# Placing the output scatters of the last layer of a four-layer graph network

## The chip, the cores and the metric

One core of one Trainium2 chip runs the whole kernel as one program. The metric is the device time of one execution in microseconds (us); the time before is the median of three executions, 2123.89 us.

## The reference, cut to what matters

The input x holds 16 samples of 1024 nodes with 128 features, adj is a 1024 x 1024 adjacency matrix in which about 0.8% of the entries are set. Four layers follow each other. Layers 0, 2 and 3 are attention over the neighbours of a node with 8 heads of 16 features, then a residual, a layer norm, a two-layer feed-forward of width 256, a residual and a layer norm. Layer 1 is graph attention with one score per edge.

```python
def attention(adj, h):                        # layers 0, 2, 3
    Q, K, V = h @ Wq, h @ Wk, h @ Wv          # 8 heads of 16
    scores = where(adj == 0, -inf, Q K^T / 4)
    o = softmax(scores) V
    x = layer_norm(h + o @ Wo + bo)
    return layer_norm(x + relu(x @ W1 + b1) @ W2 + b2)

def graph(adj, x):                            # layer 1
    h = x @ W
    e = leaky_relu((h @ a_src)[i] + (h @ a_dst)[j])
    return layer_norm(softmax(where(adj == 0, -inf, e)) @ h + x)
```

## The kernel before

**Tiling.** The graph is sparse, so the kernel gathers the neighbours of a node and does not multiply with the whole matrix. At the start (graph, slots) it sorts the nodes by degree and makes lists of neighbours. A layer is cut into 16 blocks: two groups g of 8 samples, and for each of them eight sets t of 128 nodes (in four quarters of 32). The list units holds the 64 blocks of all layers in order; a block is called by its index there, so blocks 48 to 63 are the last layer.

**Parts.** A block of an attention layer has five parts. A part is one or two chunks; a chunk is one gather of 128 table rows (4 neighbours for each of 32 nodes), and a row holds keys and values of 8 samples, 8 KB. The five parts have 2, 2, 2, 1 and 2 chunks. The one chunk of the fourth part mixes neighbours of all quarters that were left over. Sets t = 1 and t = 4 have pairs whose two chunks belong to the same quarter.

**The loop.** The loop over i goes through all 288 parts in order. begun is the index of a block's first part, so that i == begun + 3 is its fourth. In an iteration i of an attention layer the instructions are issued in this order:

- products(i), L985: VectorE multiplies the gathered keys with the queries, 128 x 2048 for two chunks. In the fourth part GpSimd does it instead (product_of_shared, L1000), issued two iterations ahead.
- summed(i - 2), L1062: TensorE sums the weighted values of neighbours into the nodes. In the second part of a block, divided starts for the block before (the denominators, also L1062).
- exponentials(i): VectorE sums over the 16 features of a head (L1018), ScalarE takes exponentials (L1022).
- weighted(i - 1), L1046: VectorE multiplies values with exponentials, in the same buffer.
- gathered(i - 1 + AHEAD) with AHEAD = 4, L971: GpSimd issues the indirect DMAs of the part three ahead, into one of four buffers e, the one that weighted(i - 1) has just read.
- product_of_shared(i + 2) on GpSimd, if that is a fourth part.
- all output scatters that stand in the list ready, on GpSimd (L702). Behind them the small addition of the sums to seen (L1115), in the iteration after the division.
- in the second part: the division of the block before (L1099, L1102 on VectorE), which makes its two tails, one for each half h of 4 samples.

**Tails.** A tail (attention_tail, then finish) does the output projection, the norms and the feed-forward of one half on TensorE and ScalarE, in small steps that are put between the parts above by a plan written out by hand (PLANS). It starts in the second part of the block after its own and is done in the second part of the next. At its end in the last layer, finish turns the half into the tile outs (two buffers, tag kv), and when the second half is there it puts one scatter of both halves into ready: 128 rows of 4 KB to the places of the nodes in out.

**The end.** The tails of block 63, the last, run after the loop with nothing beside them; half 1 uses VectorE where half 0 uses ScalarE. finish scatters each half by itself (L695), with the row numbers in halves, which are made at the start (L394). The scatter of block 62 is issued after the loop as well, ahead of block 63's tails.

**Queues.** All indirect DMAs are issued from GpSimd's queue in program order; the plain ones (x from kept, qx from qr) from SyncE's.

Of the kernel before, what the change touches and what calls it, by code (L numbers as in the profile page):

```python
# [16 lines left out]
I32 = mybir.dt.int32  # L17
AF = mybir.ActivationFunctionType
ALU = mybir.AluOpType
# [3 lines left out]
P = 128  # L23
# [20 lines left out]
T = N // P  # L44
GR = 2
G = B // GR
HF = 2
# [97 lines left out]
def sparse_path(ctx: ExitStack, tc: tile.TileContext, a: dict, out: bass.AP, flag):  # L145


    nc = tc.nc
    const = ctx.enter_context(tc.tile_pool(name="const", bufs=1))
# [25 lines left out]
    def rep_of(j, whole=False):  # L175
# [6 lines left out]
            name=nc.get_next_instruction_name(), act_func_set_id=BOTH,  # L182
# [9 lines left out]
    marks = const.tile([P, len(MARK), 32], F32, name="marks")  # L192
    nc.gpsimd.memset(marks, 0.0)
    places = const.tile([P, GR, T], I32, name="places")
    halves = const.tile([P, HF], I32, name="halves")
    bad = const.tile([P, T], F32, name="bad")
    seen = const.tile([P, 2, G * H], F32, name="seen")
    nc.gpsimd.memset(seen, 0.0)
# [37 lines left out]
    def graph(wide):  # L236
# [146 lines left out]
        there = s1.tile([P, T], F32, name="there")  # L383
# [5 lines left out]
        for g in range(GR):  # L389
            nc.vector.tensor_scalar(  # L390
                places[:, g, :], there, float(GR), float(g), ALU.mult, ALU.add,
            )
        for h in range(HF):
            nc.vector.tensor_scalar(  # L394
                halves[:, h : h + 1], there[:, T - 1 :], float(GR * HF), float((GR - 1) * HF + h),
                ALU.mult, ALU.add,
            )
        low = s1.tile([P, T], F32, name="low")
        nc.vector.tensor_tensor(bad, sorted_[:, :, 2], caps[:, :T], ALU.is_gt)
# [251 lines left out]
    def turned(z, dst, gain=None, shift=None, dve=False):  # L651

        ps = bank([P, GH, P])
        for i in range(GH):
            nc.tensor.transpose(ps[:, i, :], z[:, i, :], ident)  # L655
        if dve and gain is None:
            nc.vector.tensor_copy(dst, ps)
        elif dve:
            nc.vector.tensor_scalar(dst, ps, gain, shift, ALU.mult, ALU.add)
        elif gain is None:  # L660
            nc.scalar.copy(dst, ps)  # L661
        else:
            nc.scalar.activation(dst, ps, AF.Identity, bias=shift, scale=gain)  # L663
# [5 lines left out]
    ready = []  # L669

    def finish(l, g, t, h, z, gain, shift, dve=False):
        if l + 1 < len(LAYERS):

            wanted[0] = True
            while held[0]:
                advance(slow)
            wanted[0] = False
            busy[0] += 1
            xn = states.tile([P, GH, P], F32, tag="xT", name="xT")
            turned(z, xn, gain, shift)  # L680
            yield "free"
            yield from project(l + 1, g, t, h, xn)
            busy[0] -= 1
            return
        xn = states.tile([P, GH, P], F32, tag="xT", name="xT")
        turned(z, xn, gain, shift, dve)
        yield
        if h == 0:
            leaving[g, t] = twos.tile([P, HF, GH, D], F32, tag="kv", name="outs")
        o = leaving[g, t]  # L690
        turned(xn, o[:, h], dve=dve)
        yield
        yield
        if (l, g, t) == units[-1]:
            nc.gpsimd.indirect_dma_start(  # L695
                out=out.rearrange("n (k c) -> (n k) c", k=GR * HF),
                out_offset=bass.IndirectOffsetOnAxis(ap=halves[:, h : h + 1], axis=0),
                in_=o[:, h].rearrange("p g d -> p (g d)"), in_offset=None,
            )
        elif h + 1 == HF:  # L700
            rows = o.rearrange("p h g d -> p (h g d)")
            ready.append(lambda: nc.gpsimd.indirect_dma_start(  # L702
                out=out.rearrange("n (k c) -> (n k) c", k=GR),
                out_offset=bass.IndirectOffsetOnAxis(ap=places[:, g, t : t + 1], axis=0),
                in_=rows, in_offset=None,
            ))

    def hidden():
        return ones_.tile([P, F * GH * P], F32, tag="f1", name="f1")
# [157 lines left out]
    units = [(l, g, t) for l in range(len(LAYERS)) for g in range(GR) for t in range(T)]  # L867
# [10 lines left out]
    def is_attention(u):  # L878
        return LAYERS[units[u][0]][1] is ATTN
# [244 lines left out]
    def advance(gens):  # L1124
        for gen in list(gens):
            got = next(gen, "end")
            if got == "end":
                gens.remove(gen)
            elif got == "free":
                free.append(gen)  # L1130
# [58 lines left out]
    with tc.manual_schedule():  # L1189
        wide = [gather_buffer() for _ in range(EDGES)]  # L1190
        setup, entry, weights = graph(wide), at_once(0), load_weights("L0")
        next(setup)
        next(weights)
# [39 lines left out]
        begun = 0  # L1233
        slot = ()
        for i in range(len(parts) + 2):
            here = i < len(parts)
            u = parts[i][0] if here else len(units)
            if here:
                l = units[u][0]
                eager[0] = 1 if u < 2 else 0  # L1240
                if i and parts[i - 1][0] != u:
                    begun = i
                    if u == 1:
                        fronts.append(ends)
                    if l + 1 < len(LAYERS) and LAYERS[l + 1][1] is ATTN:
                        if units[u][1:] == (0, 1):
                            more = load_weights(LAYERS[l + 1][0])
                            next(more)
                            next(more)
                        if units[u][1:] == (0, 4):  # L1250
                            fronts.append(more)
                if is_attention(u):
                    products(i)
            if i > 1:
                summed(i - 2)
                done = parts[i - 2][0]
                if parts[i - 1 : i] == [] or parts[i - 1][0] != done:
                    closing = divided(done)
                    next(closing)
            if here and i == begun and is_attention(u):  # L1260
                shared(u)
            if here and (i == 5 or i == begun + 3 and 0 < u < T - 2):
                slot = islice(rest, 1)
                fronts.insert(0, slot)
            others()
            if here:
                exponentials(i)
                if i in (1, 6) or i == begun + 4 and 0 < u < T - 2:
                    for _ in slot:
                        pass  # L1270
                    for _ in islice(rest, 1):
                        pass
            if here and i == begun + 1:
                while loads:
                    advance(loads)
                if u + 1 < len(units):
                    fronts.insert(0 if u else len(fronts) - 1, queries(u + 1))
                loads.append(loaded(u + 2))
                if u:
                    advance(loads)  # L1280
            others()
            if 0 < i <= len(parts):
                weighted(i - 1, 0)
                if not is_attention(parts[i - 1][0]):
                    others()
                    weighted(i - 1, 2)
                gathered(i - 1 + AHEAD)
                product_of_shared(i + 2)
                while ready:
                    ready.pop(0)()  # L1290
                for _ in sizes:
                    pass
            if closing is not None and here:
                while any(gen not in free for gen in tails):
                    if opening[0] is None:
                        advance(tails)
                    else:
                        planned("ab")
                while opening[0] is not None and opening[0] < len(plan[0]):
                    planned()  # L1300
                next(closing)
                sizes, closing = closing, None
                passes = 3 if is_attention(u) else 4
                steps = STEPS if is_attention(done) else GRAPH_STEPS
                steps -= LATE[units[done][0]]
                pace[:] = 0.0, steps / (passes * sum(part[0] == u for part in parts) - 1)
                if is_attention(done) and opening[0] is None:
                    for gen in list(tails):
                        if gen in free:
                            for _ in gen:  # L1310
                                pass
                            tails.remove(gen)
                opening[0] = 0 if is_attention(done) else None
                plan[0] = PLANS.get(units[done][0], ())
            others()
            if i + 1 >= len(parts) or parts[i + 1][0] != u:

                while fronts:
                    advance(fronts)
# [445 lines left out]
```

## Time and profile before

| what | value |
|---|---|
| median of three executions | 2123.89 us (2122.29 to 2125.0) |
| the profiled execution | 2126.89 us |
| its span, first to last instruction | 2125.0 us |
| TensorE busy | 1972.9 us, 93% |
| VectorE busy | 1806.1 us, 85% |
| ScalarE busy | 1519.5 us, 72% |
| GpSimd busy | 1182.4 us, 56% |
| moved by DMA | 636.10 MB, 299 GB/s on average |
| gathers L971 | 576, 1523 ns of GpSimd each on average |
| scatters L702 | 15, 3060 ns of GpSimd in the median |
| scatters L695 | 2, 978 ns of GpSimd in the median |

In the views PE is TensorE, DVE VectorE, ACT ScalarE, POOL GpSimd; L702 is line 702 of the kernel. A timeline line gives the start in us, the duration in us, the engine, the line, the operation with its tiles as output<-inputs, and in brackets how long the engine stood idle before it and what ended that. The time of an indirect DMA on POOL is that of issuing it; the data move later. A line of the view by windows gives the window, its length, the busy us and instruction count of PE, weight loads, DVE, ACT and POOL, then the granted TensorE clock, the share of time that the DMA engines were busy, and GB/s.

### The profile page before, as it was taken

Reading aid. Unit: us, or ns where it says so; the run is one execution under the profiler, and the core shown is the slowest. Engines: PE = TensorE matmul, PEld = TensorE weight load, DVE = VectorE, ACT = ScalarE, POOL = GpSimd, SP = SyncE. Lnnn points to the kernel's source line nnn. Section 1 sums busy time; section 2 is a strip of 40 time slices with the busy share of each in tenths; the row PEclk is TensorE's granted clock in tenths of the full one; section 3 lists DMA queues with packets and bytes.
Section 4 is the critical chain, followed back from the end, with each engine's and each line's share of the span. In section 5 each row is a group of like instructions: output and inputs, shape, how many; then the busy total and the mean of one; then the engine's idle time right before and its main releaser. Section 6 shows DMA issues by size and latency. Waiting matters only on the chain.

```text
span 2125.0 us, 37303 instructions
## 1 busy us (share of the span) xinstructions
PE 1972.9 (93%) x13444; PEld 1244.8 (59%) x13444; DVE 1806.1 (85%) x1315; ACT 1519.5 (72%) x5051; POOL 1182.4 (56%) x747
## 2 busy tenths in 40 slices
PE   7689999999999999998899999999999999999986
PEld 6455665656666555554466665666656565565554
DVE  6977989999997577677899999999998898989892
ACT  3347878878786555555587887878888777777763
POOL 4344555556555488784454555555566565656550
PEclk8789999999999999999999999999999999999998
DMA  8987888889888799998899999999988878698860
GB/s 275 340 302 260 319 302 303 315 285 316 318 309 292 233 355 356 328 357 315 304 326 328 328 337 316 326 325 338 333 314 281 301 262 305 238 314 282 298 217 22
DMA packets 164800, 636.10 MB, mean 299 GB/s; under 512 B 34664, under 2 KB 37480, under 8 KB 116110
## 3 DMA queue, kind: packets, MB, share of 16 engines
q0 software_dynamic: 88720, 485.08, 64.3%
q1 hardware_dynamic: 75888, 148.57, 21.3%
q8 instruction: 108, 1.77, 0.3%
q14 instruction: 84, 0.69, 0.1%
HBM read 581.08 MB, written 92.34 MB: 317 GB/s over the span
## 4 chain that ended last, share of the span: by engine, by line
PE 49%; DVE 15%; DMA 11%; issue 9%; ACT 6%; POOL 2%; POOLq 0%; DVEq 0%; SPq 0%; ACTq 0%
PE acc L1062 13%; DMA e<-table,idx 10%; PE ps L655 5%; PE yps L755 5%; PE ps L741 5%; DVE pr L985 5%; DVE pr L1046 5%; PE ps L584 4%; DVE sc L1018 4%; PE ps L935 3%; PE yps L730 2%; PE yps L731 2%; PE yps L759 2%; PE ps L926 2%; POOL e L971 2%
## 5 line engine op out<-in xcount | busy, mean ns | idle before, releaser
L971 POOL DMA_INDIRECT e<-table,idx x576 | 877.4, 1523 | 763.2 <-DVE pr L1046 512.4
L1046 DVE TENSOR_TENSOR pr<-e,ex 128x2048 f32<-128x2048 f32 x272 | 617.7, 2280 | 76.9 <-ACT ex L1022 38.8
L985 DVE TENSOR_TENSOR pr<-e,qr 128x2048 f32<-128x2048 f32 x192 | 442.9, 2307 | 75.5 <-DMA e<-table,idx 45.1
L1062 PE MATMUL acc<-pr,marks 128*32 128x512 f32 x2200 | 437.2, 608 | 33.1 <-DVE pr L1046 19.9
L1018 DVE TENSOR_REDUCE sc<-pr 128x128 f32<-128x2048 f32 x192 | 438.9, 2286 | 6.6
L632 ACT ACTIVATE z<-yps,root 128x128 f32<-128x128 f32 x888 | 315.1, 374 | 148.3 <-PE yps L759 106.7
L755 PE MATMUL yps<-W,f 128*128 128x128 f32 x1520 | 249.7, 282 | 7.4 <-ACT f L750 5.5
L648 ACT ACTIVATE z<-yps,rstd 128x128 f32<-128x128 f32 x888 | 252.9, 370 | 3.5
L1062 PEld LDWEIGHTS acc<-pr,marks 128*32 128x32 f32 x2200 | 94.3, 110 | 266.6 <-issue 200.5
L755 PEld LDWEIGHTS yps<-W,f 128*128 128x128 f32 x1520 | 203.5, 191 | 63.0 <-ACT f L750 34.0
L584 PE MATMUL ps<-Wkv,xT 128*128 128x256 f32 x768 | 200.7, 407 | 17.4 <-ACT xT L663 8.3
L938 ACT COPY qr<-ps 128x512 f32<-128x512 f32 x384 | 204.5, 600 | 14.5 <-PE ps L935 12.9
L588 ACT COPY kv<-ps 128x512 f32<-128x512 f32 x176 | 102.7, 588 | 140.7 <-PE ps L584 121.0
L741 PE MATMUL ps<-x,W 128*128 128x512 f32 x384 | 187.2, 611 | 1.2 <-issue 0.9
L632 ACT ACTIVATION_READ_ACCUMULATOR z<-yps,root 128x1 f32 x888 | 188.1, 212 | 0.0
L584 PEld LDWEIGHTS ps<-Wkv,xT 128*128 128x128 f32 x768 | 146.5, 201 | 61.9 <-issue 14.9
L655 PE MATMUL ps<-ident,z 128*128 128x128 f32 x896 | 159.3, 290 | 23.2 <-ACT z L648 13.7
L1000 POOL TENSOR_TENSOR qx<-e,qx 128x1024 f32<-128x1024 f32 x48 | 148.4, 3092 | 57.8 <-DMA e<-table,idx 17.5
L935 PE MATMUL ps<-q,rep 32*128 32x512 f32 x768 | 151.6, 646 | 9.4 <-ACT q L930 7.4
L750 ACT ACTIVATE f<-ps,b 128x512 f32<-128x512 f32 x190 | 127.6, 694 | 44.7 <-PE ps L741 43.9
L730 PE MATMUL yps<-Wo,oT 128*128 128x128 f32 x768 | 155.2, 284 | 1.9 <-ACT oT L661 1.8
L655 PEld LDWEIGHTS ps<-ident,z 128*128 128x128 f32 x896 | 109.0, 143 | 79.6 <-ACT z L648 29.2
(178 smaller groups left out, 2851.0 us busy)
## 6 DMA issues: line engine op xcount, KB each, us to landing
table<-kv SPq DMA_DIRECT2D x88, 512.0 KB
kept<-xT SPq DMA_DIRECT2D x96, 256.0 KB
x<-kept SPq DMA_DIRECT2D x48, 512.0 KB
qx<-qr SPq DMA_DIRECT2D x54, 256.0 KB
e<-table,idx POOLq DMA_INDIRECT x576
table<-kv SPq DMA_DIRECT2D x32, 256.0 KB
qx<-qr SPq DMA_DIRECT2D x48, 128.0 KB
qx<-qr SPq DMA_DIRECT2D x12, 384.0 KB
```

Of the source, the lines that this page charges most:

```text
L584: nc.tensor.matmul(ps[:, k, :], x[:, i + k, :], w[LAYERS[l][0], "Wkv"], start=True, stop=True,)
L632: nc.scalar.activation(z[:, i, :], y[:, i, :], AF.Square, scale=D**-0.5, bias=root, accum_out=total[:, i : i + 1],)
L648: nc.scalar.activation(z[:, i, :], y[:, i, :], AF.Copy, scale=rstd[:, i : i + 1])
L655: nc.tensor.transpose(ps[:, i, :], z[:, i, :], ident)
L741: nc.tensor.matmul(ps, p["W1"][:, f * P : (f + 1) * P], x1.rearrange("p g n -> p (g n)"), start=True, stop=True,)
L755: nc.tensor.matmul(ps[:, i, :], f1[:, f, i * P : (i + 1) * P], p["W2"][:, f, :], start=(f == 0), stop=False,)
L935: nc.tensor.matmul(ps, rep_of(j), q[32 * j : 32 * j + 32], start=True, stop=True)
L971: nc.gpsimd.indirect_dma_start(out=es[i][:, k, :], out_offset=None, in_=tables[l, g][:, :], in_offset=bass.IndirectOffsetOnAxis(ap=idx[:, ...
L985: nc.vector.tensor_tensor(prs[i][0][:, :n, :], es[i][:, :n, :ROW], of_piece(qs[u], piece), ALU.mult,)
L1018: nc.vector.tensor_reduce(sc[:, :n, :], prs[i][0][:, :n, :].rearrange("p k (a d) -> p k a d", d=HD), mybir.AxisListType.X, ALU.add,)
L1046: nc.vector.tensor_tensor(prs[i][k0 // 2][:, :m, :].rearrange("p k (a d) -> p k a d", d=d), es[i][:, k0 : k0 + m, base : base + ROW].rearr ...
L1062: nc.tensor.matmul(outs[32 * j : 32 * j + 32], marks[:, mark, :], rhss, start=(chunk == mine[0]), stop=(chunk == mine[-1]),)
```

## The change

Two things are changed, both in the last layer. In the loop, scatters in ready are issued only in a block's fourth part (i == begun + 3), after that iteration's gathers; before, they were issued in whichever iteration found one, which is the second part. In finish, the last block no longer scatters each half by itself: one scatter of both halves, with the row numbers in places as for the other blocks, is issued at once when the second half is there. The tile halves and the two instructions that fill it go.

```diff
-    halves = const.tile([P, HF], I32, name="halves")
...
-        for h in range(HF):
-            nc.vector.tensor_scalar(
-                halves[:, h : h + 1], there[:, T - 1 :], float(GR * HF), float((GR - 1) * HF + h),
-                ALU.mult, ALU.add,
-            )
...
-        if (l, g, t) == units[-1]:
-            nc.gpsimd.indirect_dma_start(
-                out=out.rearrange("n (k c) -> (n k) c", k=GR * HF),
-                out_offset=bass.IndirectOffsetOnAxis(ap=halves[:, h : h + 1], axis=0),
-                in_=o[:, h].rearrange("p g d -> p (g d)"), in_offset=None,
-            )
-        elif h + 1 == HF:
+        if h + 1 == HF:
             rows = o.rearrange("p h g d -> p (h g d)")
-            ready.append(lambda: nc.gpsimd.indirect_dma_start(
+            issue = (lambda: nc.gpsimd.indirect_dma_start(
                 out=out.rearrange("n (k c) -> (n k) c", k=GR),
                 out_offset=bass.IndirectOffsetOnAxis(ap=places[:, g, t : t + 1], axis=0),
                 in_=rows, in_offset=None,
             ))
+            if (l, g, t) == units[-1]:
+                issue()
+            else:
+                ready.append(issue)
...
-                while ready:
+                while ready and i == begun + 3:
                     ready.pop(0)()
```

## The prediction, made before the changed kernel was run

> **What bounds the kernel now.** I read the page for shares first, then the chain that ended last from 1600 us on (the last layer), then VectorE's and GpSimd's timelines of one block there, the DMA share by window, and the end.
>
> ```profile
> PE 1972.9 (93%) x13444; PEld 1244.8 (59%) x13444; DVE 1806.1 (85%) x1315; ACT 1519.5 (72%) x5051; POOL 1182.4 (56%) x747
> ```
>
> No engine is full on average, so shares decide nothing. In the last layer the chain runs along DVE and, once per block, leaves it for a gather. VectorE at the end of block 62 (columns: start, us, instruction, idle before it and its releaser):
>
> ```profile
> 2024.19 2.28 DVE L1046 TENSOR_TENSOR pr<-e,ex 128x2048 f32<-128x2048 f32 x1
> 2026.39 1.21 DVE L1018 TENSOR_REDUCE sc<-qx 128x64 f32<-128x1024 f32 x1
> 2027.52 2.28 DVE L1046 TENSOR_TENSOR pr<-e,ex 128x2048 f32<-128x2048 f32 x1
> ...
> 2034.24 1.22 DVE L1046 TENSOR_TENSOR qx<-e,ex 128x1024 f32<-128x1024 f32 x1
> 2039.00 2.29 DVE L985 TENSOR_TENSOR pr<-e,qr 128x2048 f32<-128x2048 f32 x1 [3.54 <-DMA e<-table,idx]
> ```
>
> The next block's first product stands 3.54 us waiting for its two gathered row sets. The waits of DVE between 1590 and 2070 us say how regular that is: L985 waited 33.7 us for e<-table,idx in 10 cases and 11.8 in 3 cases put down to PE's L741. The three are as long as the ten and fall at the same instruction, so I take them for the same DMA wait. By block the stalls before blocks 52 to 63 are 4.46, 3.11, 3.89, 3.68, 3.42, 3.63, 3.06, 3.76, 3.75, 4.12, 3.24, 3.54: **43.66 us**, 3.64 each; before block 51 it is 1.78. The block period is 34.83 us (1620.98 to 2039.00 is twelve), DVE is busy 30.95 of it: it works without a pause save this one. GpSimd in the same block:
>
> ```profile
> 2020.48 3.69 POOL L1000 TENSOR_TENSOR qx<-e,qx 128x1024 f32<-128x1024 f32 x1
> 2024.33 3.07 POOL L702 DMA_INDIRECT out<-outs,places  x1 [0.15 <-issue]
> 2027.70 2.98 POOL L971 DMA_INDIRECT e<-table,idx  x1 [0.30 <-DVE sc L1018]
> 2030.99 1.88 POOL L971 DMA_INDIRECT e<-table,idx  x1 [0.31 <-issue]
> 2032.89 0.47 POOL L1115 TENSOR_TENSOR seen<-seen,both 128x128 f32<-128x128 f32 x1
> 2033.51 1.00 POOL L971 DMA_INDIRECT e<-table,idx  x1 [0.16 <-issue]
> 2034.82 1.50 POOL L971 DMA_INDIRECT e<-table,idx  x1 [0.30 <-issue]
> ```
>
> The two gathers at 2027.70 and 2030.99 are the ones DVE waits for. Their buffer is free when L1046 ends at 2026.47, but the scatter ahead of them on GpSimd's queue holds them. Meanwhile the DMA engines stand nearly still (second but last column is their share):
>
> ```profile
> 2026.00:2028.00 2.00, 1.48 (x12) 0.39 (x12) 2.00 (x3) 1.94 (x8) 1.70 (x2) 1.00 0.09 27
> 2030.00:2031.00 1.00, 1.00 (x10) 0.76 (x11) 1.00 (x1) 0.55 (x3) 0.69 (x2) 1.00 0.04 16
> 2031.00:2037.00 6.00, 5.88 (x31) 3.24 (x28) 4.42 (x3) 5.20 (x17) 5.21 (x5) 1.00 0.93 337
> ```
>
> So the stall comes from a late issue and not from full DMA engines.
>
> **What the Trainium skill says.** "SBUF — State Buffer", section "SBUF: two separate sides": VectorE and GpSimd share a port pair under an exclusive lock; whoever starts first keeps it for the whole instruction, and a DVE operation with two SBUF inputs locks out a GpSimd operation that reads SBUF. The trace agrees: indirect issues take 0.98 to 1.0 us alone, but the scatter of 2024.33 lies in L1046 (ends 2026.47) and ends at 2027.40, the gather of 2027.70 lies in the next (ends 2029.80) and ends at 2030.68: each 0.9 us after the DVE end. Those issued while L1018 (one input) runs are not held, nor the one of 2033.51, which began 0.73 us before a two-input one. "Perfetto Trace Analysis", section "DMA Instruction — SWDGE (GPSIMD)": the profile's end of such a DMA is that of the descriptors, not of the data. Here too: the second gather ends at 2032.87, its data let DVE go at 2038.87. "DMA: Bandwidth & Descriptors", section "Anatomy of one DMA — SWDGE (gpsimd) path": about 2.0 us fixed plus bytes at 436 GB/s. A 256 KB half scatter took 3.42 us from issue to landing here, 2.4 after its descriptors (the page's formula gives an estimate of 2.6).
>
> **Part 1: the scatter leaves the second part of the block (14 scatters).** Without it the first gather starts 0.27 us after L1046's end (as the others released by L1046 do, 2018.16 after 2017.89): at 2026.75. At that time the one-input L1018 runs, until 2027.52, so it takes 1.0 and ends at 2027.75, against 2030.68. The second starts at 2028.05, inside L1046 (to 2029.80), and ends 0.9 later, 2030.68, against 2032.87. The blocks that have no scatter yet show this very pattern:
>
> ```profile
> 1542.99 1.03 POOL L971 DMA_INDIRECT e<-table,idx  x1 [2.42 <-DVE pr L1046]
> 1544.33 2.59 POOL L971 DMA_INDIRECT e<-table,idx  x1 [0.30 <-issue]
> ```
>
> Their second ended at 1546.92, and DVE's product began at 1551.93 after a wait of 0.23: landing some 4.9 us after the last descriptor. Three readings of the new landing: both gathers shift with the first (2.93), 2035.94, stall 0.6; with the second only (2.19), 2036.68, stall 1.35; 4.9 us after 2030.68, 2035.58, stall 0.25. DVE is ready at 2035.46. I take a rest of 0.7, with 0.25 and 1.35 as ends. Gain 12 x (3.64 - 0.7) = **35.3** (27.5 to 40.7). Before block 51 the second gather is held by L1046 anyway; only the scatter's 0.5 MB leaves its way: 0.7 (0 to 1.8).
>
> **Part 2: the scatter enters the fourth part.** There it follows the two gathers of the next block's second part and precedes those of its third. The two before it come earlier than now: the small addition L1115 then falls in L985 and takes some 1.6 us (as at 1614.43), the gathers run from about 2032.5 to 2034.8 (now 2036.3). The scatter starts near 2035.1, in the short L1046 (2034.24 to 2035.46), and ends near 2036.4. Queued behind it: two gathers, which then meet the next block's L985 (2036 to 2038.4) and end near 2039.3 and 2040.6 instead of 2038.9. Their reader is the third product, now at 2054.30, then about 2051.4. The slowest pair in the trace landed 8.8 us after its first descriptors' end, here 2048.1: 3 us to spare, and it covers the 0.5 MB of the scatter (1.4 us at the 380 GB/s of busy windows). Cost 0; without this cover, its lateness less 3 us for each block. The gather of the fourth part waits for a later L1046 and not for GpSimd. The outs buffer is one of two and is rewritten a block later: no wait. SP's queue is not passed.
>
> **Part 3: what is late next.** TensorE. Its waits in one period (1992.2 to 2026.5) add up to about 5 us: 2.1 in L935, 1.3 before L1062, the rest behind ScalarE. From that point to the last denominator matmul it runs 21.2 us, and DVE's reciprocal L1099 comes 26.0 after it, 23.1 with the stall shortened: 1.9 us of cover. That suffices in most blocks. In blocks whose pieces take two chunks of one quarter (t = 1 and 4: blocks 52, 57, 60) L1062 needs more: 3.62 us instead of 1.91 at 1580.87, and the reciprocal after it, in a block without scatter, waited 3.14 us for PE. Four such pieces, 1.7 each, less part of the cover: I charge **4** (0 to 20).
>
> **Part 4: the end.** Now:
>
> ```profile
> 2113.41 0.69 DVE L657 COPY outs<-ps 128x512 f32<-128x512 f32 x1 [0.84 <-PE ps L655]
> 2113.76 0.99 POOL L695 DMA_INDIRECT out<-outs,halves  x1 [26.47 <-ACT outs L661]
> 2117.98 0.97 POOL L695 DMA_INDIRECT out<-outs,halves  x1 [3.23 <-DMA out<-outs,halves]
> ```
>
> The second half's scatter waits for the first to land, since both write out. One scatter starts after both halves are there, 2114.10 + 0.27 = 2114.4, ends at 2115.4, lands 2.4 + 0.7 later (0.26 MB more at 380 GB/s), 2118.5. Now it is 2118.95 + 2.4 = 2121.4. Gain **2.9** (2 to 3.5). The two L394 instructions (0.15 each, at 52 us) go; counted as 0. The scatter of block 62 at 2085.77 comes after the loop and stays.
>
> **Sum.** 35.3 + 0.7 - 4 + 2.9 = 34.9. The profiled execution took 2126.89 (span 2125.0), so it would take 2092.0; the runs' median is 3.0 lower, 2123.89, which gives **2089.0**.
>
> **Rivals.** *TensorE takes over in every block.* For it: PE is busy 33.6 of 34.8, and the only blocks without scatter had that 3.14 us wait. Against it: some 5 us of its busy time and gaps are waits, several of them behind DVE. If each reciprocal waits 1.7 us: 34.9 + 4 - 20.4 = 18.5, 2105. *The landing does not move*, since the DMA engines are slow at that time for another reason: only the end's 2.9 stay, 2121. Against it: shares of 0.09 and 0.04. That the scatter isn't moved at all, because an output becomes ready after the fourth part, would look the same; but all 14 are issued in the second part today, so they are ready. *Slower: the third part's gathers come late.* Delayed by the scatter, its data and the lock, they make the third product wait x in each block; it decides from x = 2.9, a landing at 2054.3. At x = 4: 2123.9 + 48 - 34.9 = 2137. Against it: needs 6 us more than computed; for it: DMA share is 0.8 already.
>
> **Chances.** Forecast 0.70, TensorE 0.17, no move 0.05, slower 0.08. The best ends (0.25 left, PE 0, block 51 in full) give 40.7 + 1.8 + 2.9, some 45: 2079; the range goes to 2112, past the TensorE case. A measurement of this kernel tells 0.2% (4.2 us) from no change: faster 0.87, same 0.05, slower 0.08.
>
> **What would show it.** L702 of about 1.3 us near the end of each block, after two gathers; L971 released by L1046 starting 0.3 us after it and taking 1.0; the wait of L985 for e under 1 us at block starts; L1099 waiting for PE after blocks 52, 57, 60 only; one scatter at the end, with no wait for out. I am wrong if the third or second product of a block begins to wait for e, or L1099 in every block.

## The result and the profile after

The changed kernel takes **2100.33 us** (median of six executions, 2096.53 to 2106.7), the kernel before beside it 2124.31 (2122.29 to 2125.0): ratio **0.9896**, 95% interval 0.9877 to 0.9914, 24 us faster. The profiled execution is the fastest of the six: 2096.53 us, span 2094.6, against 2126.89 and 2125.0 before. Between the two profiles lie 30.4 us. The six executions differ by 10 us and those of the kernel before by 3; but in the experiments below the kernel before itself, run 31 times, ranges from 2117.23 to 2131.91 us, so the wider spread is not shown to come from the change.

```profile
PE 1948.5 (93%) x13444; PEld 1236.2 (59%) x13444; DVE 1805.4 (86%) x1313; ACT 1518.2 (72%) x5051; POOL 1149.2 (55%) x746
```

VectorE does the same work (1805.4 us against 1806.1) in a shorter span. Line numbers have moved: L977 is the product that was L985, L1010 the sum (L1018), L1038 the weighting (L1046), L963 the gather (L971), L992 GpSimd's product (L1000), L690 the scatter. VectorE in block 62, third part to the first product of block 63:

```profile
1996.21 2.29 DVE L977 TENSOR_TENSOR pr<-e,qr 128x2048 f32<-128x2048 f32 x1 [0.44 <-issue]
...
2004.28 2.28 DVE L1038 TENSOR_TENSOR pr<-e,ex 128x2048 f32<-128x2048 f32 x1
...
2011.00 1.22 DVE L1038 TENSOR_TENSOR qx<-e,ex 128x1024 f32<-128x1024 f32 x1
2012.55 2.29 DVE L977 TENSOR_TENSOR pr<-e,qr 128x2048 f32<-128x2048 f32 x1 [0.34 <-issue]
```

The last line answers to the one with 3.54 us of idle time before: it is 0.34 us now. GpSimd in the same stretch:

```profile
2003.50 1.03 POOL L963 DMA_INDIRECT e<-table,idx  x1 [2.42 <-DVE pr L1038]
2004.84 2.59 POOL L963 DMA_INDIRECT e<-table,idx  x1 [0.30 <-ACT rstd L632]
2007.46 1.62 POOL L1107 TENSOR_TENSOR seen<-seen,both 128x128 f32<-128x128 f32 x1
2009.23 1.01 POOL L963 DMA_INDIRECT e<-table,idx  x1
2010.54 1.00 POOL L963 DMA_INDIRECT e<-table,idx  x1 [0.30 <-issue]
2011.84 1.27 POOL L690 DMA_INDIRECT out<-outs,places  x1 [0.30 <-issue]
```

The first gather begins before the two-input L1038 at 2004.28 and takes 1.03 us instead of 2.98; the second is held by it and ends 0.9 us after it; the scatter takes 1.27 us behind the next two gathers. But VectorE waits in new places, as its waits from 1590 to 2050 us say (waiter, releaser, us in total, times, longest):

```profile
DVE pr L977 <- DMA e<-table,idx: 6.6, 10, 1.1
DVE both L1091 <- PE ps L649: 5.5, 2, 3.2
DVE pr L977 <- issue: 2.9, 6, 0.8
DVE sc L1010 <- POOL qx L992: 2.3, 1, 2.3
```

And GpSimd's product of the fourth part waits for its gathered rows, 26.2 us in 11 blocks; before, it did so once, for 2.3:

```profile
POOL qx L992 <- DMA e<-table,idx: 26.2, 11, 4.6
```

To compare kernels I took the time from the first product of block 51 to that of block 63 ("twelve blocks") from VectorE's timeline and added up what VectorE loses in it. "First" is the idle time before the first products of blocks 52 to 63, "second" and "third" that before the second and third products of blocks 51 to 62. "Late fourth" is idle time of L1010 behind GpSimd's product of the fourth part, plus what the two-input operations that write pr take over their usual 2.28 us (counted where over 0.1), since GpSimd holds the port then. "Other" is mostly the reciprocal behind PE. All are in us, one profile for each kernel; those below the first two are explained in the next section.

| kernel | twelve blocks | first | second | third | late fourth | other | sum |
|---|---|---|---|---|---|---|---|
| before | 418.0 | 43.7 | 0 | 0 | 1.1 | 0 | 44.7 |
| after | 392.5 | 2.1 | 2.3 | 4.4 | 5.7 | 3.3 | 17.7 |
| loop_only | 395.0 | 2.3 | 2.2 | 6.8 | 6.5 | 2.0 | 19.8 |
| end_only | 417.4 | 42.1 | 0 | 0 | 1.6 | 0.5 | 44.2 |
| old_place_little | 419.4 | 44.5 | 0 | 0 | 1.4 | 0.5 | 46.4 |
| old_place_sync | 389.1 | 4.4 | 0 | 0 | 9.3 | 1.1 | 14.8 |
| part3 | 403.7 | 4.1 | 18.6 | 1.3 | 4.8 | 0.5 | 29.3 |
| part5 | 393.5 | 0.8 | 0 | 1.4 | 14.9 | 3.0 | 20.1 |
| part1 | 388.8 | 1.2 | 0 | 2.1 | 8.3 | 4.0 | 15.5 |
| no_scatter | 390.4 | 5.8 | 0.6 | 1.4 | 7.3 | 0.8 | 16.0 |
| after_again | 396.9 | 4.6 | 2.4 | 5.3 | 7.4 | 2.6 | 22.3 |
| part1_again | 392.8 | 2.3 | 0 | 1.2 | 10.7 | 4.0 | 18.2 |
| after_x_late | 396.2 | 17.1 | 1.1 | 1.5 | 1.2 | 1.7 | 22.6 |
| part1_x_late | 395.4 | 17.3 | 0 | 0 | 2.7 | 1.9 | 21.9 |

Without these losses the blocks take nearly the same everywhere: 418.0 - 44.7 = 373.3 before, 392.5 - 17.7 = 374.7 after (from unrounded times), 373.0 to 375.2 in all fourteen. Two profiles of the changed kernel, after and after_again, differ by 4.4 us, so differences of that size between kernels say nothing.

### The profile page after: what moved, and what is told of

Same layout as the page of the kernel before. It is cut to its first block, busy times and chain, and to the rows that moved or that the text cites. A ratio compares the mean times of both kernels' runs of the same rounds, so it can differ in the third digit from the quotient of the medians.

```text
span 2094.6 us, 37299 instructions
## 1 busy us (share of the span) xinstructions
PE 1948.5 (93%) x13444; PEld 1236.2 (59%) x13444; DVE 1805.4 (86%) x1313; ACT 1518.2 (72%) x5051; POOL 1149.2 (55%) x746
## 4 chain that ended last, share of the span: by engine, by line
PE 53%; issue 12%; DMA 11%; ACT 10%; DVE 9%; POOL 3%; POOLq 0%; DVEq 0%; SPq 0%; ACTq 0%
PE acc L1054 14%; DMA e<-table,idx 8%; PE yps L747 6%; PE ps L649 6%; PE ps L733 5%; PE ps L578 4%; DVE pr L1038 4%; PE ps L927 3%; PE yps L751 3%; PE yps L723 3%; ACT z L626 3%; PE yps L722 2%; DVE pr L977 2%; ACT qr L930 2%; PE ps L918 2%
## 5 line engine op out<-in xcount | busy, mean ns | idle before, releaser
L963 POOL DMA_INDIRECT e<-table,idx x576 | 860.8, 1494 | 748.8 <-DVE pr L1038 485.5
L1038 DVE TENSOR_TENSOR pr<-e,ex 128x2048 f32<-128x2048 f32 x272 | 613.1, 2264 | 87.8 <-ACT ex L1014 41.9
L977 DVE TENSOR_TENSOR pr<-e,qr 128x2048 f32<-128x2048 f32 x192 | 444.8, 2317 | 42.2 <-ACT qr L930 16.5
L1010 DVE TENSOR_REDUCE sc<-pr 128x128 f32<-128x2048 f32 x192 | 438.9, 2286 | 6.6
L642 ACT ACTIVATE z<-yps,rstd 128x128 f32<-128x128 f32 x888 | 253.0, 370 | 3.5
L992 POOL TENSOR_TENSOR qx<-e,qx 128x1024 f32<-128x1024 f32 x48 | 141.2, 2943 | 73.7 <-DMA e<-table,idx 37.6
L649 PE MATMUL ps<-ident,z 128*128 128x128 f32 x896 | 154.1, 287 | 21.3 <-ACT z L642 12.1
L723 PE MATMUL yps<-centre,x 128*128 128x128 f32 x768 | 152.5, 280 | 1.9
L927 PE MATMUL ps<-q,rep 32*128 32x512 f32 x768 | 142.4, 646 | 9.3 <-ACT q L922 8.3
```

The costliest lines, as they stand in the source:

```text
L642: nc.scalar.activation(z[:, i, :], y[:, i, :], AF.Copy, scale=rstd[:, i : i + 1])
L963: nc.gpsimd.indirect_dma_start(out=es[i][:, k, :], out_offset=None, in_=tables[l, g][:, :], in_offset=bass.IndirectOffsetOnAxis(ap=idx[:, ...
L977: nc.vector.tensor_tensor(prs[i][0][:, :n, :], es[i][:, :n, :ROW], of_piece(qs[u], piece), ALU.mult,)
L1010: nc.vector.tensor_reduce(sc[:, :n, :], prs[i][0][:, :n, :].rearrange("p k (a d) -> p k a d", d=HD), mybir.AxisListType.X, ALU.add,)
L1038: nc.vector.tensor_tensor(prs[i][k0 // 2][:, :m, :].rearrange("p k (a d) -> p k a d", d=d), es[i][:, k0 : k0 + m, base : base + ROW].rearr ...
```

## The experiments

**My theory**: the scatter's slot on GpSimd's queue (the time for which its issue occupies GpSimd), made long by the port lock, held the gathers of the next block's first part; what is left after the change are waits that a shorter block brings. **Rivals**: the scatter's 0.5 MB in the DMA queues did it, not the slot; the end did more than 3 us; TensorE bounds the shorter block.

**The two parts apart.** loop_only takes the condition alone:

```diff
-                while ready:
+                while ready and i == begun + 3:
```

> Only the move of the 14 scatters to the fourth part; the last block still goes out in two half scatters. If the two edits are separate, as I hold, this gives the layer's gain without the end's: the changed kernel's 2100.3 plus about 3, some 2103.5, with the same wait of 3.2 us of the second half scatter at the end. If the end's scatter mattered more than its 3 us (rival), it would be over 2106.

Measured 2104.51 us, ratio 0.9891 (0.9845 to 0.9937). The second half scatter waits for the first again, 2.88 us. end_only is the changed kernel with that line as it was.

> Only the single scatter at the end; the 14 scatters are issued as soon as they are ready, in the second part. By my sum 2124.3 - 3.1 = 2121.2, and the waits of the first product of each block for e stay at some 3.6 us each. The rival that part of the layer's gain came from elsewhere would show below 2118.

Measured 2122.50, ratio 0.9991 (0.9976 to 1.0007); the first product's waits are all there (42.1 us in twelve). The gain is the loop's; the end's few us can't be told from nothing by time, though the profiles show them (below).

**Slot or data.** Both variants keep the scatters' old time. old_place_little leaves the slot and takes the data away (64 bytes per row):

```diff
+            few = (lambda: nc.gpsimd.indirect_dma_start(
+                out=out.rearrange("n (k c) -> (n k) c", k=GR * ROW // 16),
...
+                in_=rows[:, :16], in_offset=None,
+            ))
+            issue = whole if (l, g, t) == units[-1] else few
```

> As end_only (scatters in the second part), but each of the 14 moves only 64 bytes for each row, to other rows of the output, so the output is not the reference's. GpSimd's slot and the port lock stay, the data go. If the slot causes the stall, as I hold, the first product still waits 2.5 to 3.6 us in each block and the time is 2105 to 2121, near end_only. If the 0.5 MB ahead of the gathers in the DMA queues causes it (rival), the wait falls under 1 us and the time comes to about 2095.

Measured 2124.07, ratio 0.9994 (0.998 to 1.0008). GpSimd and the product it delays (line numbers shift by kernel; the scatter is L695 here, the gather L969, the product L983):

```profile
1991.29 3.08 POOL L695 DMA_INDIRECT out<-outs,places  x1 [0.16 <-issue]
1994.67 2.98 POOL L969 DMA_INDIRECT e<-table,idx  x1 [0.30 <-DVE sc L1016]
1997.95 1.87 POOL L969 DMA_INDIRECT e<-table,idx  x1 [0.31 <-issue]
```

```profile
2006.09 2.29 DVE L983 TENSOR_TENSOR pr<-e,qr 128x2048 f32<-128x2048 f32 x1 [3.68 <-PE ps L739]
```

A scatter of 8 KB takes GpSimd the same 3.08 us as one of 512 KB, and the stall is what it was. (This stall, put down to PE, sits among those put down to the DMA and is as long: the one before it, at 1971.32, is 4.12 us.) old_place_sync does the reverse:

```diff
+            plain = (lambda: nc.sync.dma_start(
+                out[t * P : (t + 1) * P, g * ROW : (g + 1) * ROW], rows
+            ))
+            issue = whole if (l, g, t) == units[-1] else plain
```

> As end_only, but the 14 outputs leave by a plain DMA of the same 512 KB from SyncE's queue, to rows in sorted order, so the output is not the reference's. The data stay at the old time, GpSimd's slot goes. If the slot causes the stall, the first product's wait falls under 1 us and the time is about that of the changed kernel, 2095 to 2103. If the data cause it (rival), the waits stay near 3.6 us and the time near 2121.

Measured 2096.59, ratio 0.9867 (0.9835 to 0.9899). VectorE's first products of two blocks in it (L981 here):

```profile
1975.38 2.29 DVE L981 TENSOR_TENSOR pr<-e,qr 128x2048 f32<-128x2048 f32 x1
...
2007.36 2.29 DVE L981 TENSOR_TENSOR pr<-e,qr 128x2048 f32<-128x2048 f32 x1 [0.53 <-PE ps L649]
```

All the bytes, no slot, and the stall is gone in eleven of twelve blocks; before block 58 VectorE still waits 3.35 us, of which more under no_scatter. So the slot is the cause, and the data rival falls.

**Which place.** Each is the changed kernel with another part in the condition: begun + 2, begun + 4 and begun. These runs and all that follow met other chips, on which the kernel before takes 2113 to 2115 us instead of 2124 to 2125, so ratios are compared.

> The changed kernel with the scatters issued in the third part, after the gathers of the next block's first part and before those of its second part. The slot theory: the first product's wait stays away (under 1 us), as nothing stands ahead of its gathers, but the second product's gathers come 1.5 to 3.4 us later, and they follow the first ones closely in the DMA queues, so L977 waits for e in second place in most blocks by 1 to 2.5 us: 2108 to 2120. Rival, that any place behind the first part's gathers does as well: 2096 to 2105.

Measured 2094.86, ratio 0.9914 (0.9893 to 0.9935). The second product now waits, 18.6 us in all, as the slot theory says; that is 1.5 per block, inside the expected 1 to 2.5. The time alone does not decide: by ratio it would be 2106 us beside a kernel before of 2124, just under the expected 2108 to 2120 and just over the rival's 2096 to 2105, and the interval covers the changed kernel's ratio.

> The changed kernel with the scatters issued in the fifth part, behind the third part's gathers too. If the third product's waits of 0.4 to 1.1 us after the change come from the scatter ahead of its gathers, they go here; the scatter's 0.5 MB then stands ahead of the fourth part's gather, whose GpSimd product may start later and hold the port against L1038. Net 2095 to 2102. Rival, that the third product waits for another reason (full DMA engines): the waits stay, 2098 to 2104.

Measured 2086.33, ratio 0.9866 (0.984 to 0.9892). The third product's waits fall to 1.4, the late fourth part rises to 14.9: both halves of the expectation.

> The changed kernel with the scatters issued in the first part of the next block, behind the fourth part's gather as well; block 61's output then leaves after the loop with block 62's. If the scatter is what makes the fourth part's gather late, and with it GpSimd's product, the long L1038 of 2.7 to 3.3 us and GpSimd's waits for e before L992 (26 us in all after the change) go too: about 2092 to 2097. Rival, that these come from the shorter block alone: they stay, 2096 to 2102.

Measured 2084.02, ratio 0.9855 (0.9834 to 0.9876): of the three places the lowest time, though not told apart from part5. On GpSimd the scatter falls into a pause here, and nothing is held (so in all 13 blocks that issue one in the loop):

```profile
1909.78 2.79 POOL L963 DMA_INDIRECT e<-table,idx  x1 [2.63 <-DVE pr L1038]
1912.88 1.02 POOL L690 DMA_INDIRECT out<-outs,places  x1 [0.30 <-issue]
1916.50 1.01 POOL L963 DMA_INDIRECT e<-table,idx  x1 [2.60 <-DVE pr L1038]
```

But the reason that I had expected fails: GpSimd still waits for the fourth part's rows, 21.1 us where the changed kernel has 26.2.

```profile
POOL qx L992 <- DMA e<-table,idx: 21.1, 8, 5.0
```

> The changed kernel without the 15 scatters of the loop (only the last block's output is written, so the output is not the reference's). It is the floor for any place of them: neither slot nor data. I expect the third product's waits gone, GpSimd's waits before L992 reduced but not gone, 2088 to 2095. The rival, that TensorE bounds the blocks once the first wait is gone, gives the same as the changed kernel within 3 us, 2097 to 2103, with L1091 waiting for PE.

Measured 2083.17, ratio 0.9861 (0.9839 to 0.9883): no faster than part1, so there the scatters cost nothing that can be measured. The late fourth part stays here too (7.3 us), so the scatter is not needed for it; it is largest in part5 (14.9), where the scatter stands right ahead of the fourth part's gather. TensorE does not take over: "other" is 0.8. One block shows the stall with no scatter near:

```profile
1826.40 3.15 POOL L963 DMA_INDIRECT e<-table,idx  x1 [3.37 <-issue]
1838.54 2.29 DVE L977 TENSOR_TENSOR pr<-e,qr 128x2048 f32<-128x2048 f32 x1 [4.24 <-DMA e<-table,idx]
```

The first gather of block 58 began 0.03 us after a two-input L1038 (1826.37) and not ahead of it as usual, was held to 0.9 us after its end, and VectorE lost 4.24 us. In old_place_sync the same happened in the same block (a gather of 3.15 us, a wait of 3.35). Why the gather came late there the profiles don't show. It supports the account: a gather that starts inside the two-input operation is enough for a stall of this size, and the scatter made that the rule.

**Why the fourth part is late.** The DMA share in the first 20 us of a block, in the 4 us after, and in the rest (columns as before: the last two are share and GB/s; the share adds up the time that packets took, so it can pass 1), first the kernel before, then after:

```profile
2004.36:2024.36 20.00, 19.60 (x135) 12.18 (x133) 19.79 (x12) 15.55 (x50) 8.71 (x6) 1.00 0.93 317
2024.36:2030.96 6.60, 5.73 (x42) 2.93 (x40) 6.60 (x4) 5.02 (x20) 6.02 (x2) 1.00 0.32 125
2030.96:2039.00 8.04, 7.92 (x43) 4.76 (x40) 4.46 (x4) 6.03 (x22) 6.83 (x6) 1.00 0.93 322
```

```profile
1884.10:1904.10 20.00, 19.37 (x147) 13.36 (x146) 18.96 (x12) 15.19 (x49) 9.91 (x7) 1.00 1.01 361
1904.10:1908.10 4.00, 4.00 (x34) 1.99 (x34) 4.00 (x3) 3.67 (x14) 1.58 (x2) 1.00 0.43 178
1908.10:1916.43 8.33, 8.21 (x47) 4.28 (x41) 8.21 (x5) 7.75 (x29) 7.24 (x6) 1.00 0.81 287
```

After the change the DMA engines are busy without a pause in the 20 us in which the fourth part's gather has to land. Over all twelve blocks the mean share of their first 20 us is 0.925 before and 0.982 after. To test whether that backlog is the reason, the 512 KB of x, issued 7 to 9 us into each block (1892.60 in the block shown), were moved into the gap:

```diff
+            if here and u >= 46 and i == begun + 3:
+                for _ in loaded(u + 2):
+                    pass
...
-        nc.sync.dma_start(
+        queue = nc.scalar if u >= 48 else nc.sync
+        queue.dma_start(
```

They ran with two repeats for comparison on the same chip.

> The changed kernel once more, beside the variants of its scatter's place on the same chip and with a new profile. Ratio to the kernel before 0.988 to 0.992. In the last layer GpSimd's product of the fourth part (L992) waits for e in most blocks and some L1038 or the sum L1010 behind it are late, as in the first profile.

Measured 2093.36, ratio 0.9912 (0.9893 to 0.993), as expected.

> Scatters in the first part of the next block, beside the changed kernel on the same chip: faster than it by 0.3 to 0.5%, if the waits of the third product after the change come from the scatter ahead of its gathers. If the place behind those gathers makes no difference: within 0.1% of the changed kernel.

Measured 2083.05, ratio 0.9853 (0.9833 to 0.9874): 10 us below the changed kernel (0.5%, as expected), intervals apart, so part1 **is** faster. But the two profiles do not show that the place is why. Of the 7.9 us between their spans, 6.9 were there before the last layer, where the two kernels are the same: its first product began at 1508.51 in after_again and at 1501.64 here. From there to the end they took 580.7 and 579.7 us. (In the first profile of part1 that stretch took 573.0, in the first of the changed kernel 575.8.)

> The changed kernel with one transfer moved: in the last layer the 512 KB of x from kept are issued from ScalarE's queue in the fourth part, where the DMA engines have room (share 0.2 to 0.4), instead of from SyncE's some 5 us into the block, where they are full. If a backlog in the DMA queues makes the fourth part's gather late, GpSimd's waits for e before L992 fall from 26 us to under 15 and the long L1038 and the third product's waits shrink: 5 to 10 us faster than the changed kernel. If the gather is late for its issue or its wait for the buffer (rival), nothing changes but the issues on ScalarE, 0 to 3 us slower.

Measured 2091.81, ratio 0.9897 (0.9875 to 0.9918): not told apart from the changed kernel; the expected 5 to 10 us did not come. But the profile moved as the backlog theory says (L993 is L992 there):

```profile
POOL qx L993 <- DMA e<-table,idx: 7.3, 6, 1.8
```

In after_again, the repeat of the changed kernel, this was 26.7. The late fourth part fell from 7.4 to 1.2 us, the third product's waits from 5.3 to 1.5, the mean share of the first 20 us from 0.98 to 0.92. The first product's waits rose from 4.6 to 17.1: its gathers are issued as before (1.03 and 2.59 us) but VectorE starts on their rows 5.5 to 7.7 us after the last descriptor (in after_again 4.7 to 5.3 in eleven of thirteen blocks): the 512 KB now stand ahead of them. All losses together stayed, 22.3 and 22.6. The transfer changed its queue as well as its time; a change of queue alone was not run.

> Both: scatters in the first part, x from kept in the fourth part from ScalarE's queue. With the backlog theory the losses left in the first variant (GpSimd's late product 8 us, third product 2 us) shrink by half: 3 to 7 us faster than that variant. Rival as before: the same within 2 us, or a later bound by TensorE, with L1091 waiting for PE in more blocks.

Measured 2087.08, ratio 0.9879 (0.9857 to 0.9901), no gain over part1_again: late fourth from 10.7 to 2.7, first product from 2.3 to 17.3. The waits moved as the backlog theory says, the expected gain failed: bytes moved out of one full stretch delayed the gathers of the next.

## Why the prediction was right, and where it was not

- **What bounds the layer**: right, and shown: the slot alone brings the stall, the data alone don't.
- **Part 1**, the gathers' new times: right to a few tenths (1.03 and 2.59 us, as in the blocks without scatter). The waits left before the first product, forecast at 0.7 each, 8.4 us, are 2.1: the landing is the third of the prediction's readings, 4.9 us after the last descriptor. This part gained 41.6 us, not 35.3.
- **Part 2**, "Cost 0", with "3 us to spare": this step failed. It took 8.8 us, called the slowest, from a pair's first descriptors to its landing. (Counted the same way, the pair of block 52 had taken 9.1 in the same trace.) These were pairs of a first part, which are issued while the DMA engines stand nearly still (shares of 0.09 and 0.04 in block 62). The third part's pair has two other pairs and the scatter ahead of it. In block 59 of the changed kernel its first descriptors ended at 1887.29, and VectorE began at 1900.32 after a wait of 0.83: 13.0 us, some 4 more than assumed. In the six blocks in which VectorE waited for such a pair it was 12.7 to 13.8. The third product's waits add up to 4.4 us (6.8 in loop_only); they are 0 to 2.1 in the kernels with the scatter elsewhere or nowhere. The second product's 2.3 I had not seen either; they are gone in part1 and part5. By the prediction's own sign, "I am wrong if the third or second product of a block begins to wait for e", this part was wrong, and its rival "slower" came near: the landing was 4 of the 6 us later that it needs.
- **What is late next**: I named TensorE and charged 4; its reciprocal waits are 2.4 us, all in block 58. Of the three blocks named (52, 57 and 60; the sum counts four pieces) only 57 was followed by one. What I left out is GpSimd's product: its gather lands later in a shorter block, it starts while VectorE needs the port, 5.7 us instead of 1.1. Both costs have to do with one quantity that I read but did not carry into the sum, the share of the DMA engines outside the stall (0.93 from 2031 to 2037).
- **The end**: forecast 2.9. Count from VectorE's last norm step z<-yps,rstd to the end of the span: before, L642 at 2109.35, 15.65; now L636 at 2082.05, 12.55. That is 3.1.

```profile
2086.24 0.69 DVE L651 COPY outs<-ps 128x512 f32<-128x512 f32 x1 [1.52 <-PE ps L649]
...
2087.70 0.98 POOL L690 DMA_INDIRECT out<-outs,places  x1 [26.60 <-DVE flag L1335]
```

  One scatter and no wait for out. It began 0.77 us after the copy, not 0.27; from its start to the end of the span it is 6.9 us, as for the half before (7.0), so the larger transfer's 0.7 did not show.
- **The sum**: forecast 31.3 for the twelve blocks, measured 418.0 - 392.5 = 25.6. It is made of a gain of 41.6 before the first products, less 14.6 of new waits (4 were charged) and 1.4 of blocks that are longer for no reason found. So two errors partly cancelled. Block 50 gave 0.9 (0.7), the end 3.1 (2.9); the remaining 0.8 of the 30.4 lies in the last block and its tails. The median was forecast at 2089.0 and is 2100.3, 11.3 more: 4.5 are what the profiled execution missed of its 2092.0, 3.8 its distance from its own median, being the fastest of six, and 3.0 that the profiled execution before was above its median. That the range reached 2112 and so holds 2100.3 is luck in part: it was stretched to take in a TensorE case that did not come, and not for the waits that did.

## What to carry to other kernels

Before moving a DMA issue, ask which instruction stands behind it on its queue and who reads that: here 8 KB cost as much as 512 KB, because the slot held the next gather. Then look where the DMA engines have room after the gain: here the first 20 us of the shorter block left them hardly any, and moving 512 KB out of them was paid by the gathers behind. A time to landing read after a quiet stretch is not that of a gather with others ahead of it. Look, too, for a place where GpSimd waits anyway: in part1 the scatter held nothing there, and that kernel ran faster than the changed one, though its profiles don't show that the place is the reason.

## What the runs showed of the hardware

- An indirect issue is held only if it starts inside a two-input VectorE operation on SBUF tiles. In the kernel before, after 1500 us, 74 began inside one and ended 0.85 to 0.94 us after it (so they took 1.5 to 3.07 us); the 89 others took at most 1.03. Bytes don't count: 3.08 us for 8 KB, 3.07 for 512 KB. L1102, one of whose two inputs (acc) lies in PSUM, holds none. The edge is sharp: begun 0.04 us ahead of L1046 (1611.21 against 1611.25) an issue took 1.01 us; in no_scatter, begun 0.03 us behind L1038, it took 3.15. A few begun up to 0.04 us behind were not held (0.99 us at 1875.95 after the change).
- The Trainium skill, "SBUF — State Buffer", section "SBUF: two separate sides", has the first to start keep the port pair for its whole instruction. For GpSimd's own two-input product the runs agree: in part1 L992 ran from 1727.68 to 1730.03, and the L1038 begun at 1728.01 took 4.18 us instead of 2.28. One case goes the other way: in part1_again an L977 begun at 1619.09 took 5.01 us, though the L992 that ran from 1619.57 to 1621.94 had begun after it. For an indirect issue they do not: before the change one ran from 1985.11 to 1986.10, and the L985 begun at 1985.33 took its usual 2.28.
